# Two graph layers over 4096 nodes on one core: a reciprocal moved behind the first key group, and eleven value tiles written beside the rank sort

## The chip, the cores and the metric

The kernel runs on one core of a Trainium2 chip. A core has five engines that work at the same time, each through its own queue in order: TensorE (PE in the profile, PEld its weight loads), VectorE (DVE), ScalarE (ACT), GpSimd (POOL) and SyncE (SP, which only issues transfers here). They share 16 DMA engines. The metric is the device time of one execution in microseconds (us), as the median of several runs.

## The reference

All numbers are float32. `x` is 4096 x 512, `adj` 4096 x 4096 with very few ones (a chance of 0.000976562 for each entry, made symmetric, with the diagonal set). There are two layers, cut here to what matters:

```python
# layer 0
h = jnp.maximum(_layernorm(x), 0.0)
Q, K, V = (h @ W.T for W in (WQ, WK, WV))       # 8 heads of 64
attn = Q.K / 8 + (Q @ we.T + be)                # per head; only where adj > 0
hard = (attn == max over neighbours) / HEADS
x = x + hard @ V                                # the winning neighbour's values
# layer 1
h = jnp.maximum(_layernorm(x), 0.0)
agg = mask @ h / deg
x = x + relu(concat(h @ W_self + b_self, agg @ W_nb + b_nb) @ W_comb + b_comb)
```

So layer 0 picks for every node and head the neighbour with the best score and adds its values. Layer 1 sums the rows of all neighbours.

## The kernel before, in words

A tile is 128 nodes, so there are 32 (`KT`). The sparse path keeps a table `K_d` in device memory with one row for each node: values V (512 columns), keys K (512), a list of up to 24 neighbours with metadata, and the row of x.

*Stage A, the rows in their own order.* `x` and `adj` are streamed tile by tile. Each tile gets its layernorm, its transposed normalized rows (`hT`, kept in a large buffer `room`, tag `hT_R`), keys, and its neighbour list out of packed adjacency words. The 15 odd tiles below 31 (`EARLY_V`) get their values as they pass. The other 17 are `late_v`: their `hT` stays in `room` and their values are multiplied later. `room` also lends three spare stretches to the stream for rows of `adj`; the third begins at `END_R` and has 2048 columns.

*Ranks.* At the end of stage A (L1000 to L1083) the nodes are sorted by degree, with one-hot products on TensorE. `perm` (L1083) holds the sorted order. `more_values(n)` (L999) writes `n` late tiles here: four matmuls each into `pv` (L627; the profile has two records for one), a scaling copy on ACT into `vs` (L833), and a transfer into the V columns of `K_d`. Before the change it writes 4 tiles behind the rank's prefix sums and 1 behind the rank products (`SOON` is 5), from a pool of three buffers. Those 12 tiles that come after the ranks have had zeros written into their V columns first by SP (L992), since a gather could touch them.

*Stage B, 32 turns.* The loop from L1521 runs from i = -5 to 31 with one sorted tile a turn. Turns are of two kinds. In an `apart` turn the gathers fetch keys only, and the winners' values are fetched later by eight gathers (`value_gathers`, `o`). In a `fused` turn the gathers fetch keys and values together, and the winners' values are picked on DVE. The tiles with most neighbours come first; turns 0 to 3 are apart, later the kinds alternate, and the last ones are fused. A turn uses the engines so:

- POOL: indirect gathers by line 1097, first the row tile (`km`, five turns ahead), then one gather for each neighbour slot (`kg`, or `room` in a fused turn), then value gathers.
- PE: transposes (L1132), the query `q` (L627), and the products `pg` (L627) and `pr` (L1343, L1345) of layer 1.
- DVE: `xo` (L1283: row plus winners' values), then `scores` over key groups, a first of one slot and then of four (multiply L1218, reduce L1221), then the winners (L1237 to L1276).
- ACT: the statistics of `xo` up to the square root of the variance (L1290 to L1293), and the normalization `layer1_norm` (L1310 to L1314).

The layer-1 work of a tile is spread over four turns by the table `plan`: statistics and norm at turn i, transpose at i + 1, products at i + 2, and at i + 3 the `move`: ACT copies `pg` into `gs` (L1351), DVE writes `own` (L1357, called inside `scores` behind the first group of four), and POOL scatters `gs` into `G_d` (L1113). From turn 28 on, two tiles' statistics share a turn.

The reciprocal of the deviation (L1308) is the first line of `layer1_norm`, which stands behind `winners`:

```python
if i >= 0:
    scores(turns[i], lambda: late(layer1_out, "move", i))
late(scatter, "move", i)
...
on(winners, i)
if i < KT - 2:
    late(layer1_norm, "stats", i)
```

*Order.* Both stages are under a manual schedule: the instructions of each engine stand in the order of the program, and semaphores between them follow from reads and writes of the same data. For gathers and writes that touch different columns of `K_d`, `declare_no_dep` says so: the list `beyond` holds gathers that skip the V columns, the list `written` the value writes.

*Stage C, the dense part.* The first eight sorted tiles (`DENSE`) are summed by matmuls over all rows of `G_d` (`da`, L1637); the other tiles gather `G_d` and reduce on DVE. Output follows.

Of the kernel before, what the change touches and what calls it, by code (L numbers as in the profile page):

```python
# [9 lines left out]
F32 = mybir.dt.float32  # L10
# [8 lines left out]
P = 128  # L19
D = 512  # L20
# [517 lines left out]
def sparse_path(  # L538
# [4 lines left out]
    nc = tc.nc  # L543
    N = x.shape[0]
    KT = N // P
# [36 lines left out]
    late_v = [t for t in range(KT) if t not in EARLY_V]  # L582
    RING = 3
    SOON = 5
    room = wp.tile([P, KT * D], F32, tag="hT_R", name="room")
    HALF_R = KT * D // 2

    def hT(t):
        if t in EARLY_V:
            at = EARLY_V.index(t) % RING * D  # L590
        else:
            k = late_v0.index(t)
            at = (RING + k) * D if k < SOON else HALF_R + (k - SOON) * D
        return room[:, at : at + D].rearrange("p (c q) -> p c q", q=P)

    late_v0 = list(late_v)

    END_R = HALF_R + (len(late_v) - SOON) * D
    spare = [
        room[:, at : at + N // 2]  # L600
        for at in (HALF_R - N, HALF_R - N // 2, END_R)
    ]
    assert (RING + SOON) * D <= HALF_R - N and END_R + N // 2 <= KT * D

# [24 lines left out]
    with ExitStack() as pa:  # L629
# [7 lines left out]
        psm = pa.enter_context(tc.tile_pool(name="spsm", bufs=4, space=PSUM))  # L637
# [3 lines left out]
        st = [dict() for _ in range(KT)]  # L641
# [183 lines left out]
        def values(t, ps):  # L825
            pv = ps.tile([P, D], F32, tag="pm", name="pv")
            project(pv, hT(t), ws["wv"])
            return pv

        def values_out(t, pv, pool, eng):  # L830
            vs = pool.tile([P, D], F32, tag="gs", name="vs")

            nc.scalar.activation(vs, pv, AF.Copy, scale=1.0 / H)  # L833
            return eng.dma_start(K_d[ts(t, P), 0:D], vs)
# [111 lines left out]
        for t in range(KT):  # L946
# [30 lines left out]
            if t - 1 in BATCHES[1:]:  # L977
                if decoding:
                    decode_some(99)
                k = BATCHES.index(t - 1)  # L980
# [4 lines left out]
        for b in range(4):  # L985
            n = (KT - FROM_X) * P // 4
# [3 lines left out]

        for t in late_v[SOON:]:
            nc.sync.dma_start(K_d[ts(t, P), 0:D], zero)  # L992
# [2 lines left out]
            nc.sync.dma_start(b, bias.rearrange("(c p) -> p c", p=P))  # L995
        load_fold(1)
        l3.close()
        fo = pa.enter_context(tc.tile_pool(name="sfo", bufs=3))

        def more_values(n):  # L1000
            for t in late_v[:n]:
                values_out(t, values(t, psm), fo, nc.scalar)
            del late_v[:n]


# [32 lines left out]
        )  # L1038
        for k in range(2):
            nc.vector.tensor_tensor(acc[:, ts(k, HF)], pps[k], acc[:, ts(k, HF)], ALU.add)  # L1040
        more_values(4)
        nc.vector.tensor_tensor(acc, acc, ohf, ALU.mult)
        nc.vector.tensor_reduce(
            degc, acc.rearrange("p (b t) -> p t b", b=BINS), AX.X, ALU.add
# [27 lines left out]
        for t in range(KT):  # L1072
            nc.tensor.matmul(
                pp, ohp[:, t, :], tk[:, t], start=(t == 0), stop=(t == KT - 1)
            )
        more_values(SOON - 4)
        decode_some(99)
        words_top(KT - 1)
        decoding = decode(BATCHES[-2], KT - BATCHES[-2])
# [6 lines left out]
    with ExitStack() as pb:  # L1086
# [5 lines left out]
        psm = pb.enter_context(tc.tile_pool(name="spsm2", bufs=3, space=PSUM))  # L1092
# [11 lines left out]
                for w in written:  # L1104
                    tc.declare_no_dep(last[0].ins, w.ins, reason="other columns")

        written, beyond = [], []

        def put_rows(dst, r, src):
            if puts and puts[-1] is last[0]:  # L1110
# [25 lines left out]
        st = [dict() for _ in range(KT)]  # L1136

        def rows(r):

            if r in wide:  # L1140
                k = (wide.index(r) + 3) % OWNS
                own = big[:, OWN0 + k * VKX : OWN0 + (k + 1) * VKX]
                gather(own, K_d[:, :], perm[:, r : r + 1])
                km = own[:, D:VKX]
                st[r]["own"] = own
            else:
                km = xp.tile([P, ROWX], F32, tag="km", name="km", bufs=8)
                gather(km, K_d[:, :], perm[:, r : r + 1], D)
            st[r].update(km=km, xg=km[:, M_X:ROWX])
# [62 lines left out]
        def scores(r, within):  # L1212

            s = st[r]
            sc = bp.tile([P, LIST, H], F32, tag="sc", name="sc", bufs=1)
            for kk, g0, g in s["kg"]:
                pr = bp.tile([P, GRP, D], F32, tag="pr", name="pr", bufs=1)
                nc.vector.tensor_tensor(  # L1218
                    pr[:, :g, :], s["q"].unsqueeze(1).to_broadcast([P, g, D]), kk, ALU.mult
                )  # L1220
                nc.vector.tensor_reduce(  # L1221
                    sc[:, g0 : g0 + g, :],
                    pr[:, :g, :].rearrange("p g (h d) -> p g h d", h=H), AX.X, ALU.add,
                )
                if g0:
                    within()
                    within = lambda: None
            s["sc"] = sc
# [50 lines left out]
        def layer1_stats(r, by_vector=False):  # L1279
# [21 lines left out]
            nc.scalar.activation(rs, v, AF.Sqrt)  # L1301
            s.update(xo=xo, mv=mv, v=v, rs=rs)

        def layer1_norm(r):
            s = st[r]
            if "sq" in s:
                xo, q = s["xo"], s["sq"]
                nc.vector.reciprocal(q[:, 4:5], q[:, 2:3])  # L1308

                nc.scalar.activation(q[:, 5:6], q[:, 4:5], AF.Square)  # L1310
                nc.scalar.activation(q[:, 5:6], q[:, 5:6], AF.Identity, bias=three, scale=q[:, 3:4])
                nc.scalar.activation(q[:, 6:7], q[:, 4:5], AF.Copy, scale=q[:, 5:6])
                nc.scalar.activation(q[:, 7:8], q[:, 6:7], AF.Copy, scale=q[:, 0:1])
                nc.scalar.activation(s["hn"], xo, AF.Relu, bias=q[:, 7:8], scale=q[:, 6:7])  # L1314
                return
            xo, mv, v, rs = (s[k] for k in ("xo", "mv", "v", "rs"))
            nc.vector.reciprocal(rs, rs)

            newton(nc, bp, v, rs, 1, 1)
            nb = bp.tile([P, 1], F32, tag="nb1", name="nb1")  # L1320
            nc.vector.scalar_tensor_tensor(nb, mv[:, 0:1], -1.0, rs, ALU.mult, ALU.mult)
            hn = bp.tile([P, D], F32, tag="hn1", name="hn1", bufs=3)
            nc.scalar.activation(hn, xo, AF.Relu, bias=nb, scale=rs)
            s["hn"] = hn
# [68 lines left out]
        def fold_bias():  # L1393
            for pm in biased:
                nc.vector.tensor_tensor(bb, pm, bb, ALU.add)
# [29 lines left out]
        turns = apart[:FIRST]  # L1425
        left, last_tiles, m = apart[FIRST:], fused[-3:], KT - FIRST - 3
        n = m - len(left)
# [7 lines left out]
        OWNS = (KT * D - OWN0) // VKX  # L1435


        wide = [r for r in fused if r not in last_tiles and pos[r] > 7]
# [19 lines left out]
        i = 0  # L1458
        while ready:
            ripe = sorted(e for e in ready if e[0] <= i)  # L1460
            for e in ripe[: 2 if i >= KT - 4 else 1]:
                ready.remove(e)
                r = e[2]
# [15 lines left out]
        def late(step, kind, i, *args):  # L1479

            out_ = []
            for r in turns:
                if plan[kind].get(r) == i:
                    out_ += step(r, *args) or []
            return out_
# [22 lines left out]
        for i in range(-5, KT):  # L1508


            if i == -3:
                load_fold(0)
            if i == 0:
                load_bias()
            if i == 1:
                wS = wp.tile([P, NC, D], F32, tag="w_b", name="swS")
                wN = bp.tile([P, NC, D], F32, tag="swN", name="swN", bufs=1)
            a, b = on(key_gathers, i), late(value_gathers, "value", i)
            while a or b:
                for q, n in ((a, max(1, round(len(a) / max(1, len(b))))), (b, 1)):  # L1520
                    for g in q[:n]:  # L1521
                        gather(*g)
                    del q[:n]
            on(rows, i + 5)
            late(layer1_move, "move", i)
            on(query_copy, i + 2)
            late(layer1_copy, "layer1", i)
            early = [r for r in tail if plan["turn"][r] == i - 1]
            for r in early:
                tail_turn(r)  # L1530
            if i >= 0 and turns[i] in fused:
                own_values(turns[i])
            late(layer1_stats, "stats", i, i >= KT - 2)
            if i >= KT - 2:
                late(layer1_norm, "stats", i)
            on(query_norm, i + 4)
            on(query, i + 1)
            for part in between.get(i, ()):
                fold(*part)
            late(layer1, "layer1", i)  # L1540
            for r in early:
                tail_product(r)
            if i in (-1, 0):
                n = 6 if i < 0 else KT
                for t in late_v[:n]:
                    w = values_out(t, values(t, psm), bp, nc.sync)
                    for g in beyond:
                        tc.declare_no_dep(w.ins, g.ins, reason="other columns")
                    written.append(w)
                del late_v[:n]  # L1550
            if i == max(between) + 1:
                fold_bias()
            if i >= 0:
                scores(turns[i], lambda: late(layer1_out, "move", i))
            late(scatter, "move", i)
            if i == KT - 2:
                wg = dense_words()
                gsl = [gp.tile([P, GRP, D], F32, tag="kg", name="gs") for _ in range(2)]
# [3 lines that stand above are left out]
            on(query_turn, i + 3)  # L1562
            late(layer1_turn, "turn", i)
            for r in early:
                tail_move(r)
# [14 lines left out]
        r = 0  # L1580
        while r < KT:
# [6 lines left out]
            r = e  # L1588
# [17 lines left out]
    with ExitStack() as pd:  # L1606
# [83 lines left out]
        for r in range(DENSE, KT):  # L1690
            n = CAPS[r] - 1
# [68 lines left out]
```

## Time and profile before

| what | value |
|---|---|
| median of three runs | 1306.7 us (1304.51, 1306.7, 1310.19) |
| the profiled execution's own time | 1449.11 us |
| its span, and mean granted TensorE clock | 1447.4 us, 0.859 |
| DVE layer-1 wait at turn 3: idle before the reciprocal at 515.17 us | 31.68 us, released by ACT L1292 |
| L627 `pv`, all 256 matmuls: busy, mean | 119.0 us, 617 ns |
| L1097 `kg` gathers, 177: busy, mean | 170.1 us, 961 ns |
| L1637 `da`, 512 matmuls: busy, mean | 241.8 us, 628 ns |

The profiled execution is 142 us longer than the median. In the profile's clock row a 9 stands for a slice in which TensorE had full clock; where the digit is lower, its matmuls run longer. A row of the timeline gives start, busy time, engine, line and operation; in square brackets stand the idle time of the engine before it and what ended that. A "L" number is a line of the kernel before.

### The profile page before, as it was taken

To read this page: it belongs to the slowest core of one execution; us is meant where nothing else is said; L and a number is where in the kernel's file an instruction comes from. 1 tells how busy PE (TensorE), PEld (TensorE's weight loads), DVE (VectorE), ACT (ScalarE), POOL (GpSimd) and SP (SyncE) were. 2 spreads that over 40 slices of the span, in tenths; PEclk is the share of its full clock that TensorE was granted. 3 is DMA by queue.
4 is the path that set the end of the run, shared out by engine and by line. 5 is a ranking of instruction groups with operands and counts; after the bars stand their busy time and mean duration, and the time that the engine had idled before them with its cause. 6 is when DMAs were issued, how large, how long until landed. Compare 5 with 4: busy or idle time off the path is not lost. (4 is left out here: it accounts for less than half of the span.)

```text
span 1447.4 us, 10779 instructions
## 1 busy us (share of the span) xinstructions
PE 1053.6 (73%) x2918; PEld 484.7 (33%) x2918; DVE 994.0 (69%) x1666; ACT 420.9 (29%) x862; POOL 773.9 (53%) x910
## 2 busy tenths in 40 slices
PE   5998989565495457666787719466978597996972
PEld 3554555232142123222233303122433243442431
DVE  5568786984566279887787749566764464964985
ACT  5787768311020043223233304233431000000000
POOL 2322322236627666666766665466443757574774
PEclk9999999886798678878888868788999898996985
DMA  9999998396735567777877775576652997575873
GB/s 364 420 419 420 420 357 314 121 331 198 209 108 153 149 197 227 226 234 228 234 228 234 211 240 171 181 219 194 197 182 93 307 347 254 196 257 186 275 260 114
DMA packets 109222, 350.09 MB, mean 242 GB/s; under 512 B 18064, under 2 KB 18064, under 8 KB 100960
## 3 DMA queue, kind: packets, MB, share of 16 engines
q0 software_dynamic: 63376, 208.23, 46.5%
q1 hardware_dynamic: 40416, 131.35, 23.5%
q10 hardware_dynamic: 5360, 9.73, 2.0%
q8 instruction: 25, 0.41, 0.1%
q14 instruction: 45, 0.37, 0.1%
HBM read 285.25 MB, written 68.19 MB: 244 GB/s over the span
## 5 line engine op out<-in xcount | busy, mean ns | idle before, releaser
L1637 PE MATMUL da<-gk,mk 128*128 128x512 f32 x512 | 241.8, 628 | 51.0 <-issue 36.1
L627 PE MATMUL pg<-swN,hT 128*128 128x512 f32 x216 | 124.0, 728 | 130.7 <-ACT hT L1332 99.9
L1097 POOL DMA_INDIRECT room<-G_d,sidx x174 | 176.7, 1016 | 56.5 <-issue 51.8
L1097 POOL DMA_INDIRECT kg<-K_d,sidx x177 | 170.1, 961 | 64.4 <-issue 52.1
L1221 DVE TENSOR_REDUCE sc<-pr 128x32 f32<-128x2048 f32 (+3 forms) x114 | 183.3, 1608 | 3.9
L627 PE MATMUL q<-wq,hqT 128*128 128x512 f32 x256 | 130.7, 639 | 56.6 <-issue 55.0
L1637 PEld LDWEIGHTS da<-gk,mk 128*128 128x128 f32 x512 | 102.2, 200 | 190.5 <-issue 190.5
L1659 DVE TENSOR_REDUCE acc<-room 128x512 f32<-128x4096 f32 (+5 forms) x23 | 152.3, 6623 | 5.4 <-DMA room<-G_d,sidx 3.9
L1097 POOL DMA_INDIRECT o<-K_d,vi x128 | 123.4, 964 | 60.5 <-issue 60.5
L627 PE MATMUL pv<-wv,room 128*128 128x512 f32 x256 | 119.0, 617 | 18.4 <-ACT vs L833 18.4
L627 PE MATMUL pk<-wk,room 128*128 128x512 f32 x256 | 121.0, 617 | 4.1 <-ACT room L809 4.0
L1097 POOL DMA_INDIRECT room<-K_d,sidx x102 | 97.7, 958 | 42.4 <-issue 24.4
L1218 DVE TENSOR_TENSOR pr<-q,kg 128x2048 f32<-128x2048 f32 (+3 forms) x51 | 102.4, 2007 | 25.2 <-DMA kg<-K_d,sidx 24.1
L627 PEld LDWEIGHTS pg<-swN,hT 128*128 128x128 f32 x216 | 49.0, 236 | 209.9 <-ACT hT L1332 116.0
L1113 POOL DMA_INDIRECT G_d<-gs,perm x32 | 31.7, 990 | 128.6 <-ACT gs L1351 85.8
L1345 PE MATMUL pr<-swS,hT 128*128 128x512 f32 x216 | 99.9, 605 | 0.0
L1218 DVE TENSOR_TENSOR pr<-q,room 128x2048 f32<-128x2048 f32 (+3 forms) x42 | 66.8, 1590 | 43.8 <-issue 29.1
L1254 DVE COPY_PREDICATED o<-best,room 128x512 f32<-128x512 int32 x102 | 74.3, 728 | 32.4 <-issue 16.6
L627 PEld LDWEIGHTS q<-wq,hqT 128*128 128x128 f32 x256 | 49.2, 202 | 108.7 <-issue 107.0
L627 PEld LDWEIGHTS pv<-wv,room 128*128 128x128 f32 x256 | 50.4, 199 | 83.1 <-issue 62.6
L748 ACT ACTIVATE mkt<-adjt,sgb 128x2048 bf16<-128x2048 int32 x37 | 74.2, 2006 | 12.5 <-POOL adjt L669 12.2
L823 POOL DMA_DIRECT2D K_d<-ks x32 | 18.7, 585 | 98.3 <-DVE ks L818 96.1
(221 smaller groups left out, 1500.5 us busy)
## 6 DMA issues: line engine op xcount, KB each, us to landing
adjt<-adj_dram SPq DMA_DIRECT2D x37, 1024.0 KB
room<-adj_dram SPq DMA_DIRECT2D x27, 1024.0 KB
x<-X_d SPq DMA_DIRECT2D x32, 512.0 KB
xt<-x_dram SPq DMA_DIRECT2D x32, 256.0 KB
K_d<-ks POOLq DMA_DIRECT2D x32, 256.0 KB
X_d<-xo SPq DMA_DIRECT2D x32, 256.0 KB
X_d<-own SPq DMA_DIRECT2D x32, 256.0 KB
gk<-G_d ACTq DMA_DIRECT2D x16, 512.0 KB
```

Source lines behind the costliest of these rows:

```text
L627: nc.tensor.matmul(dst, h[:, c, :], w[:, c, :], start=(c == 0), stop=(c == NC - 1))
L748: nc.scalar.activation(mk, st[t]["adj"][j], AF.Sigmoid, bias=sgb, scale=400.0, accum_out=degs[:, t, j : j + 1],)
L823: nc.gpsimd.dma_start(K_d[ts(t, P), D : 2 * D], ks)
L1097: last[0] = nc.gpsimd.indirect_dma_start(out=dst, out_offset=None, in_=src, in_offset=bass.IndirectOffsetOnAxis(ap=idx, axis=0), element_o ...
L1113: new = nc.gpsimd.indirect_dma_start(out=dst, out_offset=bass.IndirectOffsetOnAxis(ap=perm[:, r : r + 1], axis=0), in_=src, in_offset=None,)
L1218: nc.vector.tensor_tensor(pr[:, :g, :], s["q"].unsqueeze(1).to_broadcast([P, g, D]), kk, ALU.mult)
L1221: nc.vector.tensor_reduce(sc[:, g0 : g0 + g, :], pr[:, :g, :].rearrange("p g (h d) -> p g h d", h=H), AX.X, ALU.add,)
L1254: nc.vector.copy_predicated(s["o"].rearrange("p (h d) -> p h d", h=H), best[:, k, :].bitcast(I32).unsqueeze(2).to_broadcast([P, H, HD]), b ...
L1345: nc.tensor.matmul(pr, s["hT1"][:, c, :], wS[:, c, :], start=False, stop=(c == NC - 1))
L1637: nc.tensor.matmul(dacc[r], masks[s][:, h, r, :], keys[s][:, h, :], start=(s == 0 and h == 0), stop=(s == NPL - 1 and h == 1),)
L1659: nc.vector.tensor_reduce(acc, g[:, 0:n, :].rearrange("p n f -> p f n"), AX.X, ALU.add)
```

## The change

It has three parts.

1. *Value tiles.* `more_values` now writes 8 tiles behind the prefix sums and 3 behind the rank products, 11 in all (`BESIDE`), instead of 4 and 1. They are copied into four slots of 512 columns in the third spare stretch of `room`, in turn, and no longer into the pool of three buffers. Their writes are put into `written`, so the gathers that skip the V columns need not wait for them. The six tiles left are written two a turn in turns -2, -1 and 0, where before twelve were written, six in turn -1 and six in turn 0.
2. *Reciprocal.* It leaves `layer1_norm` and becomes `layer1_inverse`. For turns below 30 it is called inside `scores`, behind the first group of four key slots and ahead of `layer1_out`.
3. *Own slots.* The formula of the slot of a fused row is written in another way; with 11 rows in `wide` it yields the same slots.

In the order of the program, DVE's eight copies of the bias (`fb`, L1372) stand ahead of `perm` (L1083) after the change.

```diff
+    BESIDE = 11
...
-        def values_out(t, pv, pool, eng):
-            vs = pool.tile([P, D], F32, tag="gs", name="vs")
+        def values_out(t, pv, pool, eng, vs=None):
+            if vs is None:
+                vs = pool.tile([P, D], F32, tag="gs", name="vs")
...
-        fo = pa.enter_context(tc.tile_pool(name="sfo", bufs=3))
+        written = []
 
         def more_values(n):
             for t in late_v[:n]:
-                values_out(t, values(t, psm), fo, nc.scalar)
+
+                at = END_R + len(written) % 4 * D
+                written.append(
+                    values_out(t, values(t, psm), None, nc.scalar, room[:, at : at + D])
+                )
             del late_v[:n]
...
-        more_values(4)
+        more_values(8)
...
-        more_values(SOON - 4)
+        more_values(BESIDE - 8)
...
-        written, beyond = [], []
+        beyond = []
...
-                k = (wide.index(r) + 3) % OWNS
+                k = (wide.index(r) - len(wide) + 4) % OWNS
...
+        def layer1_inverse(r):
+            q = st[r]["sq"]
+            nc.vector.reciprocal(q[:, 4:5], q[:, 2:3])
+
         def layer1_norm(r):
             s = st[r]
             if "sq" in s:
                 xo, q = s["xo"], s["sq"]
-                nc.vector.reciprocal(q[:, 4:5], q[:, 2:3])
...
-            if i in (-1, 0):
-                n = 6 if i < 0 else KT
+            if i in (-2, -1, 0):
+                n = 2
...
+            def within():
+                if i < KT - 2:
+                    late(layer1_inverse, "stats", i)
+                late(layer1_out, "move", i)
+
             if i >= 0:
-                scores(turns[i], lambda: late(layer1_out, "move", i))
+                scores(turns[i], within)
```

## The prediction

> **What bounds the kernel now.** I read four views in this order: the page's clock row, the waits from 330 to 430 us and from 500 to 1000 us, the timeline at the places these waits name, and sums over windows.
>
> ```profile
> span 1447.4 us, 10779 instructions
> PE 1053.6 (73%) x2918; PEld 484.7 (33%) x2918; DVE 994.0 (69%) x1666; ACT 420.9 (29%) x862; POOL 773.9 (53%) x910
> PEclk9999999886798678878888868788999898996985
> ...
> L1113 POOL DMA_INDIRECT G_d<-gs,perm x32 | 31.7, 990 | 128.6 <-ACT gs L1351 85.8
> ```
>
> No engine is full. The clock row is full for eight slices (the stage that streams adj) and ragged after. That matters for the frame: the profiled execution took 1449.11 us, the median of three is 1306.7, so 142 us of the profile are not in the runs that count. They must sit where the clock was low. The last row says that the scatters of the layer-1 products wait on ACT's copy `gs`, more than on anything else.
>
> ```profile
> POOL o L1097 <- issue: 22.1, 2, 21.8
> POOL kg L1097 <- ACT smeta L1154: 10.7, 1, 10.7
> DVE pr L1218 <- remote: 13.6, 1, 13.6
> ```
>
> ```profile
> ACT q L1310 <- DVE q L1308: 71.7, 10, 15.3
> POOL G_d L1113 <- ACT gs L1351: 63.5, 9, 14.9
> DVE q L1308 <- ACT q L1292: 31.7, 1, 31.7
> ```
>
> The first three rows are 330 to 430 us, the others 500 to 1000 us (total, times, longest). At the start of the turns POOL stands still for 21.8 us before the first value gather: it needs all V rows written. Later ACT waits ten times for the reciprocal (71.7 us) and POOL nine times for `gs` behind it.
>
> ```profile
> 298.40 13.90 PE L627 MATMUL pv<-wv,room 128*128 128x512 f32 x32
> 425.42 0.95 POOL L1097 DMA_INDIRECT o<-K_d,vi  x1 [21.77 <-issue]
> ...
> 704.11 0.29 ACT L1292 ACTIVATE q<-q,c 128x1 f32<-128x1 f32 x1
> 716.86 0.15 DVE L1308 RECIPROCAL q<-q 128x1 f32<-128x1 f32 x1
> 717.04 0.20 ACT L1310 ACTIVATE q<-q 128x1 f32<-128x1 f32 x1 [11.40 <-DVE o L1254]
> ...
> 1035.48 0.21 DVE L1308 RECIPROCAL q<-q 128x1 f32<-128x1 f32 x2
> 1037.82 0.69 DVE L1283 TENSOR_TENSOR xo<-km,o 128x512 f32<-128x512 f32 x1 [2.13 <-ACT hn L1314]
> 1039.70 0.56 ACT L1351 COPY gs<-pg 128x512 f32<-128x512 f32 x1
> 1040.55 1.00 POOL L1113 DMA_INDIRECT G_d<-gs,perm  x1 [8.22 <-ACT gs L1351]
> 1058.09 1.00 POOL L1113 DMA_INDIRECT G_d<-gs,perm  x1 [9.01 <-ACT gs L1351]
> ```
>
> The first line gives the price of a value tile at full clock: 13.90 / 4 = 3.47 us. The square root of a turn is ready at 704.40, its reciprocal runs at 716.86, because it stands behind the winners. At 1035 the chain reciprocal, norm on ACT, `gs`, scatter is plain, and DVE's next `xo` waits for it too.
>
> ```profile
> 449.00:1018.00 569.00, 352.54 (x829) 148.68 (x828) 406.50 (x495) 166.42 (x433) 369.82 (x385) 0.80 0.70 210
> 1018.00:1114.00 96.00, 80.75 (x213) 35.30 (x212) 62.00 (x121) 31.50 (x75) 35.02 (x42) 0.95 0.46 157
> 1114.00:1447.00 333.00, 263.76 (x560) 110.25 (x558) 221.59 (x110) 0.00 (x0) 210.77 (x216) 0.87 0.72 242
> ```
>
> Columns: window, length, busy PE, PE load, DVE, ACT, POOL (and counts), clock, DMA share, GB/s. In the middle turns POOL comes nearest to full: an indirect DMA is 0.95 to 0.96 us and 0.30 before the next, 1.257 us apiece, so 384 x 1.257 = 482.7 of 569 us.
>
> **What the Trainium skill says.** "TensorE: Matmul & The Clock Gate", What's actually happening: TensorE starts at half clock and returns to it after an idle window of about 3.4 us. The trace agrees that waits and low clock go together (clock 0.80 in the middle turns), but a low stretch costs more here than a factor of two: one value tile ran from 360.9 to 381.9 and the next to 396.6, 21.0 and 14.7 us against 3.47. "Perfetto Trace Analysis", Tensor Engine Instruction (MATMUL, LD_WEIGHTS): a matmul's end is estimated, and ACT, DVE and GpSimd are strict FIFO. It fits: records of `pv` end near 363 us while ACT's copy waits until 381.9, and `gs` stays behind a norm it has nothing to do with. "DMA: Bandwidth & Descriptors", Issuing engines are not separate DMA queues: another issuer saves only the issue time. The trace has 0.33 us (ACT) and 0.32 to 0.34 us (SP) for the value writes, so moving writes to ACT is nearly free.
>
> **The change, part by part.** The base is the profile's durations replayed at full clock, since the median is 142 us below. I split these 142: the dense end has at least (1 - 0.87) x 333 = 43 us of lost clock, call it 55 as the loss is more than linear; the start of the turns about 25; some 62 remain for 449 to 1114. POOL's idle time in the middle turns, 569 - 482.7 = 86 us, is then only 20 to 25 at full clock.
>
> *Values, start.* Before, 5 tiles run beside the ranks and 12 in turns -1 and 0 (6 and 6). After, 11 beside the ranks and 6 later, 2 a turn. The four more tiles ahead of the rank products delay TensorE: 4 tiles 298.4 to 312.3 become 8 tiles, to 326.2 (8 x 3.47 = 27.8). `r_tk`, behind eight value copies on ACT, is done about 328.1, the 1.87 us of rank products about 330. DVE's eight `fb` copies (1.18 us) now stand ahead of `perm` and still wait for the last metadata write; they ran at 332.51, so `perm` is ready at about 334.15 instead of 329.8. The first `km` gather, at 335.31 before, starts about 2.9 us after its last wait: 337.0, **+1.7 us**. The first `q` comes 5 us later (355 for 350), but turn 0 is bound by its 23 gathers, so it ends +2.9.
>
> What returns: at full clock before, 6 tiles end at 370.4, `q` of turn 1 at 374.6, the other 6 at 395.2, the last write has landed at about 400. POOL reaches its first value gather at 393.4 and waits 6.6. After, with two tiles a turn, `q` of turn 1 is done about 366 and the last write landed about 378: POOL doesn't wait. Its gathers of turn 2 end at 418.7 for 424: **-5 us**, the 1.7 included. In the profile's clock it would be some 25, as the 21.8, 10.7 and 13.6 above all hang on tiles at low clock.
>
> The slots in the adjacency's spare room replace three buffers by four: a write takes 3.3 us to land and a slot is used again after 4 x 3.47 us. I cost it at nothing; if that cover went, a tile would wait 1 to 3 us. Six fewer SP writes are worth 6 x 0.33 us on a queue nobody waits for. The own-slot formula gives the same slots, at nothing.
>
> *Reciprocal, middle turns.* 0.15 us of DVE moves from behind the winners to behind the first key group; `own` stands directly behind it. ACT gets the norm's input up to 12 us earlier (704.4 for 716.86) and the whole norm, 717.04 to 719.2 or 2.1 us, is out of `gs`'s way. Of what is late next: in the pair of turns from 694.98 to 738.21 (43.2 us), POOL has 30 DMAs, 37.7 us, and one wait for `gs`, 4.75 at 726.94, where TensorE ran at clock 0.50. There the product is late as well, and an earlier norm brings nothing to it. So at full clock these waits are small before the change, and POOL's issue is what remains. Of the 20 to 25 us left I take **-4** (bounds 0, as POOL may be full anyway, and -20).
>
> The moved reciprocal adds a wait: behind it stand `own` and the remaining key groups, and for them `scatter` doesn't wait but the next `xo` does. Its input is ready at `xo` + 3.2 to 4.4 us without trouble, the first group ends at `xo` + 6.7: no wait. Bounds 0 and +16 per turn (rival D).
>
> *Reciprocal, tail.* Window two has clock 0.95, so its waits are real in all runs. Square roots are ready at 1027.1 and 1029.1; the first group ends at 1028.8. The reciprocals come at about 1029.2 for 1035.48; norms (2 x 2.1) and `gs` 1033.8 for 1039.7. The scatter waits of 8.22 and 9.01 shrink by about 6 each, and DVE's 2.13 + 1.32 before `xo` go. What is late next is TensorE's `pg`. Half of the two 6 us reach the end, plus 3.4: **-9** (8 to 13). From i = 30 the old place stays.
>
> The dense stage has no edit: 0. Sum: -5 - 4 - 9 = -18, so 1306.7 - 18 = **1288.7, taken as 1288.5 us**. Against the profile's own execution the same steps read 25 + 25 + 12 = 62, 1449.1 to 1387, of which the median holds the 18.
>
> **Rivals.**
> A, the forecast: -18, own range 1277 to 1300.
> B, the low clock at the tiles and `gs` is in the median runs too, if less: for it speaks that every turn has TensorE pauses of several us that bring it on; against it the 142 us. Then half of the 62 and the tail's 9: -40, **1266**.
> C, the gathers' issue bounds all turns: what ACT and TensorE get earlier waits again for POOL, and two turns earlier at the start only fill slack. For it 482.7 of 569 us. What stays is half of the tail: -4, **1303**.
> D, slower: the reciprocal blocks DVE. At 483.49 DVE waited 31.68 us for the square root at its old place, with the turn's work already done. At the new place, the rest of the key groups and the winners (15 to 17 us) would come after such a wait. Two such turns cost 31, against them 18 less 3 that other waits absorb: +10 to +16, **1317**. It decides as soon as ACT's square root is later than the first group's end by over 6 us (DVE's slack: 569 - 406 = 163 us over 27 turns). Against it: the wait stands once in the profile, in a stretch of low clock.
>
> **How the numbers follow.** A 0.50, B 0.21, C 0.17, D 0.12. Half a per cent, 6.5 us, is about what a measurement of this kernel can tell from no change: 1300.2 to 1313.2. A lies almost wholly below it, B wholly; C inside it; D mostly above. Faster 0.73, same 0.16, slower 0.11. The range goes from B's lower part, 1258, to C's upper bound, 1308; left out are most of D and the lower third of B, about 0.19.
>
> **What would show it.** Right: in the profile after, POOL's wait before the first `o` gather is under 7 us; `perm` about 4 us later; the reciprocal starts within 1 us of the first group's end; the waits of ACT L1310 on the reciprocal fall to under 15 us; scatters near 1040 and 1058 wait under 4 us. Wrong: DVE waits for L1292 of over 6 us in more than two turns (D); scatter waits that stay with TensorE's `pg` as releaser (C); or a drop of over 30 us in the median (B).

## The result and the profile after

The changed kernel takes 1294.4 us (median of 4, 1291.45 to 1295.04), the kernel before 1307.7 us (median of 4) beside it. The ratio is 0.9897, 95% interval 0.9878 to 0.9916: 13.3 us less, where 18 were forecast. A ratio leaves out runs over 1.5% above the fastest of the same kernel, so it is not always the quotient of two medians.

The same kernel before has a median of 1307 us on two chips (numbers 8 and 1 in the record) and of 1442 and 1447 us on two others (0 and 4), with a lower granted TensorE clock there (0.85 to 0.86 for 0.89 to 0.90). The first profile, of 1449.11 us, is of the second kind. The runs of the result and the profile after are of the first; their chip is not on record. So before and after are compared below on a second profile of the kernel before, the run f0 (1305.33 us).

The page after, with its span, its busy row and its clock row:

```profile
span 1293.3 us, 10762 instructions
PE 1025.0 (79%) x2918; PEld 483.8 (37%) x2918; DVE 993.5 (77%) x1666; ACT 422.1 (33%) x862; POOL 776.3 (60%) x910
PEclk9999998988898868887889988988898799999985
```

Busy times are nearly those of the kernel before in its second profile (VectorE 993.8 us there, POOL 773.0, TensorE 1019.9): the change moves work. The group of scatters, from the list of groups by line (busy, mean ns, idle time ahead of them and what ended it):

```profile
L1119 POOL DMA_INDIRECT G_d<-gs,perm x32 | 32.4, 1013 | 40.0 <-ACT gs L1511 24.4 <-ACT gs L1360 8.8 <-issue 4.4
```

The scatters' idle time was 128.6 us in the first profile and is 40.0 here. But most of that fall isn't the change's. The same row of the kernel before in its second profile:

```profile
L1113 POOL DMA_INDIRECT G_d<-gs,perm x32 | 32.1, 1003 | 47.0 <-ACT gs L1502 23.8 <-ACT gs L1351 15.8 <-issue 4.8
```

It is 47.0 us: some 80 us of the first profile's waits are not there in an execution of 1305 us. The change takes the part behind the copy L1351 (L1360 after) from 15.8 to 8.8; the part behind the other copy, of the last tiles, stays (23.8 and 24.4). The waits of the changed kernel, 330 to 430 us and 500 to 1000 us:

```profile
DVE pr L1224 <- PE q L628: 26.9, 1, 26.9
POOL o L1103 <- issue: 2.7, 9, 0.3
```

```profile
ACT q L1319 <- DVE q L1312: 86.2, 23, 7.3
POOL G_d L1119 <- ACT gs L1360: 8.8, 4, 7.9
```

POOL's wait before the value gathers is gone (nine times 0.3 is the usual spacing). ACT still waits 86.2 us for the reciprocal (273.3 in the second profile before), but what matters is who waits behind it: POOL, 8.8 us. The first `q` is what VectorE now waits for longest.

The page shows what the moved reciprocal does to TensorE. The products `pg` of layer 1, before (second profile) and after:

```profile
L627 PE MATMUL pg<-swN,hT 128*128 128x512 f32 x216 | 131.6, 766 | 101.2 <-ACT hT L1332 101.2
```

```profile
L628 PE MATMUL pg<-swN,hT 128*128 128x512 f32 x216 | 97.1, 592 | 0.0
```

Before, TensorE paused 101.2 us in all ahead of `pg`, and a matmul of it took 766 ns on average; after, it doesn't pause there and a matmul takes 592 ns. The pause now stands ahead of the queries `q` (36.7 us before, 143.0 after), and they are slower instead (628 and 788 ns). The reciprocal alone does the same (run f1 below: 592 ns without a pause), and with the reciprocal moved in the late turns only (run g1) `pg` stays at 740 ns. So the pause is moved and not removed.

The tail, timeline of the changed kernel, where the forecast put most of the gain:

```profile
912.83 0.21 DVE L1312 RECIPROCAL q<-q 128x1 f32<-128x1 f32 x2
...
919.77 1.32 POOL L1119 DMA_INDIRECT G_d<-gs,perm  x1 [0.30 <-issue]
931.56 0.16 DVE L1312 RECIPROCAL q<-q 128x1 f32<-128x1 f32 x1 [2.87 <-ACT q L1298]
936.49 1.00 POOL L1119 DMA_INDIRECT G_d<-gs,perm  x1 [7.87 <-ACT gs L1360]
```

and of the kernel before in its second profile:

```profile
923.49 0.20 DVE L1308 RECIPROCAL q<-q 128x1 f32<-128x1 f32 x2
...
928.54 1.00 POOL L1113 DMA_INDIRECT G_d<-gs,perm  x1 [4.68 <-ACT gs L1351]
946.70 1.00 POOL L1113 DMA_INDIRECT G_d<-gs,perm  x1 [9.63 <-ACT gs L1351]
```

The pair of reciprocals runs 10.7 us earlier from the start of the execution, but part of that lies far ahead of it: counted from POOL's DMA 397 in the table below it is 5.7 us. The scatter behind the pair doesn't wait any more (4.68 before). The next one waits 7.87 instead of 9.63: here VectorE itself waits 2.87 us at the new place of the reciprocal.

POOL issues the same 690 indirect DMAs in the same order in all these kernels, so the start of the same one can be compared. Start times in us, from the traces (before is its second profile):

| POOL's DMA | before | values alone | reciprocal alone | both |
|---|---|---|---|---|
| last metadata write of stage A | 334.6 | 333.5 | 333.5 | 331.8 |
| indirect DMA 1, first `km` | 339.8 | 340.6 | 338.7 | 338.9 |
| 49, turn 2 | 406.2 | 404.3 | 406.7 | 403.1 |
| 397, turn 21 | 848.1 | 847.5 | 847.4 | 843.1 |
| 469, behind the scatter of turn 30 | 953.0 | 952.4 | 946.7 | 942.8 |
| span | 1303.6 | 1303.9 | 1299.0 | 1293.3 |

The first row is ahead of the change's first visible effect on POOL and differs by up to 2.8 us from run to run; differences of rows are safer than rows. Of the 10.3 us between the spans of before and both, 2.8 are in it. The steps, from before to both: metadata to `km` +1.9 (5.2 to 7.1); to DMA 49 -2.2; to 397 -1.8; to 469 -5.3; the rest -0.1. They sum to -7.5 us, against 13.3 between the medians: each column is a single execution, and the remainder isn't assigned to any stage.

### The profile page after: what moved, and what is told of

The parts are those of the page before. It is cut to its first block, busy times and chain, and to the rows that moved or that the text cites. A ratio compares the mean times of both kernels' runs of the same rounds, so it can differ in the third digit from the quotient of the medians.

```text
span 1293.3 us, 10762 instructions
## 1 busy us (share of the span) xinstructions
PE 1025.0 (79%) x2918; PEld 483.8 (37%) x2918; DVE 993.5 (77%) x1666; ACT 422.1 (33%) x862; POOL 776.3 (60%) x910
## 4 chain that ended last, share of the span: by engine, by line
DVE 21%; DMA 21%; PE 20%; POOL 19%; issue 14%; ACT 3%; SPq 0%; DVEq 0%; POOLq 0%; ACTq 0%
POOL room L1103 9%; PE pv L628 6%; DMA room<-K_d,sidx 6%; DVE pr L1224 6%; DMA room<-G_d,sidx 5%; PE pk L628 5%; POOL kg L1103 5%; DMA kg<-K_d,sidx 4%; POOL o L1103 3%; DVE sc L1227 3%; PE pr L1354 2%; PE pw L768 2%; DMA adjt<-adj_dram 2%; ACT mkt L749 2%; PE pg L628 2%
## 5 line engine op out<-in xcount | busy, mean ns | idle before, releaser
L628 PE MATMUL q<-wq,hqT 128*128 128x512 f32 x256 | 161.2, 788 | 143.0 <-DVE pr L1224 143.0
L1652 PE MATMUL da<-gk,mk 128*128 128x512 f32 x512 | 221.4, 595 | 15.8 <-DMA gk<-G_d 15.8
L1103 POOL DMA_INDIRECT room<-G_d,sidx x174 | 180.3, 1036 | 58.0 <-issue 46.3
L1652 PEld LDWEIGHTS da<-gk,mk 128*128 128x128 f32 x512 | 97.8, 191 | 139.4 <-issue 139.0
L628 PEld LDWEIGHTS q<-wq,hqT 128*128 128x128 f32 x256 | 62.5, 256 | 221.1 <-DVE pr L1224 124.2
L628 PE MATMUL pv<-wv,room 128*128 128x512 f32 x256 | 115.9, 604 | 0.0
L628 PE MATMUL pg<-swN,hT 128*128 128x512 f32 x216 | 97.1, 592 | 0.0
L1296 ACT ACTIVATE hn<-xo 128x512 f32<-128x512 f32 x29 | 18.2, 629 | 192.6 <-DVE xo L1289 185.3
L628 PEld LDWEIGHTS pk<-wk,room 128*128 128x128 f32 x256 | 48.3, 199 | 54.4 <-issue 48.8
```

The source lines that it names most:

```text
L628: nc.tensor.matmul(dst, h[:, c, :], w[:, c, :], start=(c == 0), stop=(c == NC - 1))
L1103: last[0] = nc.gpsimd.indirect_dma_start(out=dst, out_offset=None, in_=src, in_offset=bass.IndirectOffsetOnAxis(ap=idx, axis=0), element_o ...
L1296: nc.scalar.activation(junk, xo, AF.Copy, scale=-1.0 / D, accum_out=q[:, 0:1])
L1652: nc.tensor.matmul(dacc[r], masks[s][:, h, r, :], keys[s][:, h, :], start=(s == 0 and h == 0), stop=(s == NPL - 1 and h == 1),)
```

## The experiments

The first four ran on chip 0, where the kernel before takes 1442.4 us.

**The kernel before again (e0).**

> The kernel before, once more, for a profile whose clock is that of the runs that count. The theory of the prediction (full-clock replay): POOL's wait before the first value gather, 21.8 us in the first profile, is 5 to 9 us; POOL's idle time between 449 and 1018 us is 20 to 30 us instead of 86; the scatters in the tail still wait 7 to 9 us each for gs. The rival (low clock is in all runs): POOL's wait before the first value gather stays above 15 us.

It took 1452.7 us at clock 0.855, and POOL waited 18.3 us before the first value gather. This is the rival's figure, but it can't decide: the execution is of the long kind itself.

**Reciprocal alone (e1).** The kernel before with this edit only:

```diff
+        def layer1_inverse(r):
+            q = st[r]["sq"]
+            nc.vector.reciprocal(q[:, 4:5], q[:, 2:3])
...
-                nc.vector.reciprocal(q[:, 4:5], q[:, 2:3])
...
+            def within():
+                if i < KT - 2:
+                    late(layer1_inverse, "stats", i)
+                late(layer1_out, "move", i)
```

> The kernel before with the reciprocal moved and nothing else. The theory of the prediction: 9 us in the tail and 4 in the middle turns, so 1307.7 - 13 = about 1295 (ratio 0.990). Rival 1 (the values carry the gain): no change, 1304 to 1308. Rival 2 (the moved reciprocal blocks VectorE while the value tiles still crowd TensorE in turns -1 and 0): slower than before, over 1310.

Measured: 1463.8 us, ratio 1.0141 (1.0101 to 1.0181), slower. The waits of VectorE for the square root between 440 and 1000 us, with the edit and then in the kernel before (e0):

```profile
DVE q L1306 <- ACT q L1292: 121.8, 6, 42.2
```

```profile
DVE q L1308 <- ACT q L1292: 32.4, 1, 32.4
```

There are six waits for one, and from POOL's DMA 49 to its DMA 397 the turns take 553.2 us for 514.6. This fits the mechanism of rival D. But the trace is of an execution of 1495.8 us, the longest of six, so neither figure is the size of the median's loss. What is shown is that VectorE is caught at the new place; that this makes the 1.4% is argued, and the run h1 below speaks against it as the only cause.

**Values alone (e2)**, the changed kernel with the line put back:

```diff
                 xo, q = s["xo"], s["sq"]
+                nc.vector.reciprocal(q[:, 4:5], q[:, 2:3])
...
-                if i < KT - 2:
-                    late(layer1_inverse, "stats", i)
```

> The changed kernel with the reciprocal put back behind the winners. The theory of the prediction: 5 us, about 1302 (ratio 0.996). Rival 1 (the values carry the gain): 1294 to 1297. If the two single edits add up, their gains sum to the 13.3 us of the whole change.

Measured: 1457.1 us as the median of six, which scatter from 1432.1 to 1468.5. The ratio, 0.9971 (0.9906 to 1.0037), rests on two of them: no difference to be told.

**Reciprocal in the late turns (e3).**

```diff
-                if i < KT - 2:
+                if 26 <= i < KT - 2:
                     late(layer1_inverse, "stats", i)
...
-                late(layer1_norm, "stats", i)
+                late(layer1_norm, "stats", i, i < 26)
```

(The added argument makes the norm begin with the reciprocal, as before.)

> The changed kernel with the reciprocal behind the first key group in turns 26 to 29 only, behind the winners in turns 0 to 25. The theory of the prediction: the tail gives 9 of the reciprocal's 13 us, so this is some 4 us over the changed kernel, about 1298. Rival (the gain of the reciprocal lies in the middle turns): as slow as with the reciprocal put back everywhere.

Measured: 1438.2 us, ratio 0.9964 (0.9915 to 1.0012). The loss of the run with the reciprocal alone isn't there. But two things differ from that run, the reciprocal's place in the middle turns and the value tiles, so it doesn't say which of them matters.

**On a chip where the kernel before takes 1307 us.** The next three ran on chip 8 (median of the kernel before 1306.7 us), the first being the kernel before once more (f0).

> The kernel before once more. If it takes about 1307 us here, as in the runs that gave the verdict, its profile replaces the first one: POOL's wait before the first value gather 5 to 9 us, POOL's idle time between 449 and 1018 us 20 to 30 us, scatters of the tail waiting 7 to 9 us for gs. If it takes about 1440 us, this chip grants TensorE less, as in the first four runs.

It took 1305.33 us. The wait before the value gathers, timeline:

```profile
403.73 0.95 POOL L1097 DMA_INDIRECT o<-K_d,vi  x1 [6.28 <-issue]
```

It is 6.28 us, where the replay at full clock had 6.6. But from DMA 49 to DMA 397 POOL takes 441.8 us; at the 1.257 us apiece of the prediction the 348 DMAs between them are 437.4, so 4.4 us are left idle and not 20 to 30, and the longest two waits are 1.50 and 1.45. Of the two scatters in the tail one waits 4.68 us, under the 7 to 9 expected, the other 9.63.

The reciprocal alone, with the edit of e1 (f1):

> The kernel before with the reciprocal moved and nothing else, where the kernel before takes about 1307 us. The theory of the prediction: ratio 0.990 (9 us tail, 4 us middle turns). Rival 1 (the values carry the gain): 0.997 to 1.000. Rival 2 (the moved reciprocal blocks VectorE while twelve value tiles crowd TensorE and ScalarE in turns -1 and 0): over 1.005, as on the chip with less TensorE clock, where it was 1.014.

Measured: 1298.2 us, ratio 0.9927 (0.9908 to 0.9946). Both rivals are out; the gain is somewhat under the forecast 0.990. VectorE's waits for the square root between 440 and 1000 us are one of 2.8 us. In the traces POOL gains 5.6 us from DMA 397 to 469 (105.0 to 99.4) and 1.2 from 49 to 397.

The values alone, with the edit of e2 (f2):

> The changed kernel with the reciprocal back behind the winners, where the kernel before takes about 1307 us. The theory of the prediction: 0.996. Rival 1: 0.988 to 0.992. If the single edits add up, the product of both ratios is that of the whole change, 0.990.

Measured: 1306.1 us, ratio 0.9990 (0.9977 to 1.0003): no gain to be told, where 0.996 was forecast. The product of the two single ratios is 0.9917, the whole change has 0.9897; the intervals overlap. POOL's stalls in the values-alone kernel:

```profile
340.62 1.08 POOL L1103 DMA_INDIRECT km<-K_d,perm  x1 [6.30 <-issue]
367.99 0.95 POOL L1103 DMA_INDIRECT kg<-K_d,sidx  x1 [1.14 <-DVE pr L1224]
399.25 0.95 POOL L1103 DMA_INDIRECT kg<-K_d,sidx  x1 [2.65 <-issue]
```

The 6.28 us before `o` are gone; in their place stand 1.14 and 2.65 for key buffers and 1.9 more before the first `km` (6.30 for 4.42). The turns from DMA 49 to 397 also take 1.4 us more than in the kernel before (443.2 for 441.8).

The next four ran on chip 1, where the kernel before takes 1307.25 us. The first is the changed kernel with the reciprocal at its new place in turns 26 to 29 only, with the edit of e3 (g1):

> The changed kernel with the reciprocal behind the first key group in turns 26 to 29 only. Where the kernel before takes about 1307 us. If the tail carries the reciprocal's gain: within 3 us of the changed kernel, 1294 to 1297, since POOL's waits for gs between 449 and 900 us, which come back, sum to about 3 us. If the middle turns carry it: 1301 or more.

Measured: 1298.1 us, ratio 0.9925 (0.9906 to 0.9944), 3.7 us over the changed kernel's 1294.4; the intervals overlap (0.9878 to 0.9916 there). From DMA 49 to DMA 397 POOL takes 444.0 us here and 440.0 in the changed kernel. Two waits, of 2.61 and 1.80 us where the changed kernel's longest is 0.74, account for most of it. The larger:

```profile
595.96 0.99 POOL L1119 DMA_INDIRECT G_d<-gs,perm  x1 [2.61 <-ACT gs L1362]
```

So by the medians the late turns carry 8 us (1306.1 with the values alone, 1298.1 here) and the others about 4. By POOL's DMAs the late turns carry 5.4 (397 to 469: 105.0 with the values alone, 99.6 here); another 1.9 us lie behind DMA 469, a stretch that is 1.8 us longer in f1 than in f0.

**`perm` first (g2):** `fb` behind the scores of turn 0.

```diff
-            if i == 0:
-                load_bias()
...
             if i >= 0:
                 scores(turns[i], within)
+            if i == 0:
+                load_bias()
```

> The changed kernel with the eight bias copies (fb) behind turn 0's scores, so that perm no longer stands behind them. If perm behind fb costs what the prediction said: the first km gather comes 1.7 us earlier (2.8 us after the last metadata write has landed instead of 4.5), and the time is 1 to 2 us lower, 1292 to 1294. Rival (another wait takes its place): no change.

Measured: 1294.4 us, ratio 0.9903 (0.9882 to 0.9924), as the changed kernel. The first `km` comes 1.8 us sooner behind POOL's metadata write (4.5 us of idle time for 6.3), and the waits for key buffers take it back:

```profile
367.30 0.95 POOL L1103 DMA_INDIRECT kg<-K_d,sidx  x1 [2.28 <-DVE pr L1224]
399.63 0.95 POOL L1103 DMA_INDIRECT kg<-K_d,sidx  x1 [3.65 <-issue]
```

2.28 + 3.65 against 1.68 + 2.65: the rival was right.

**Eight tiles beside the ranks (g3).**

```diff
-    BESIDE = 11
+    BESIDE = 8
...
-        more_values(BESIDE - 8)
...
-            if i in (-2, -1, 0):
-                n = 2
+            if i in (-1, 0):
+                n = 4 if i < 0 else KT
```

> The changed kernel with 8 tiles beside the ranks and none behind the rank products; 4 of the other 9 in turn -1 behind the first query and 5 in turn 0. If the three tiles behind the rank products and the two of turn -2 are what holds the first query back (362.8 us in the changed kernel's profile, against 354 before): the first q is done near 352, POOL's waits of 1.7 and 2.6 us for key buffers at 365 and 395 go, no wait of over 1 us before the first value gather: 3 to 4 us lower, about 1291. Rival (turn 0's gathers hide the late query wholly): no change; or slower by the 6 us wait before the value gathers, if the last values land late.

Measured: 1292.5 us, ratio 0.9888 (0.9868 to 0.9909). The first `q` is done at 355.7 us, not near 352; in this execution the first `km` came 1.7 us later than in the changed kernel's. VectorE's first scores:

```profile
355.68 0.69 DVE L1223 TENSOR_TENSOR pr<-q,km 128x512 f32<-128x512 f32 x1 [18.11 <-PE q L628]
```

They start 15.1 us behind the first `km`; in the changed kernel it is 362.82 - 338.91 = 23.9. POOL has no wait over 0.6 us from there to the tail, and its first `o` comes 58.2 us behind `km` for 61.7. Those 3.5 us are what was expected; 1.9 show in the median, which the intervals can't separate from none.

**Turn 29 put in another order (g4).**

```diff
-                junk = bp.tile([P, D], F32, tag="hn1", name="hn1", bufs=3)
+                if r == [t for t in turns if plan["stats"][t] == KT - 3][-1]:
+                    junk = s["o"]
+                else:
+                    junk = bp.tile([P, D], F32, tag="hn1", name="hn1", bufs=3)
...
             late(layer1_move, "move", i)
+            if i == KT - 2:
+                late(layer1_norm, "stats", i - 1)
...
-            if i < KT - 2:
+            if i < KT - 3:
                 late(layer1_norm, "stats", i)
```

> The changed kernel with two edits in turn 29: the second tile's statistics use the room of its o instead of a fourth use of the three hn1 buffers, and its norms stand behind the gs copy of turn 30. If VectorE's wait of 2.9 us for the square root at 931 us and POOL's wait of 7.9 us for gs at 936 us both come from that buffer and that order: VectorE's wait goes, the scatter at 936.5 comes 3 to 7 us earlier, and the time is 3 to 5 us lower, about 1290. Rival (TensorE's products pg of turns 30 and 31 are the next wait): the scatter comes earlier, the time stays.

Measured: 1291.8 us, ratio 0.9874 (0.9852 to 0.9895), the lowest median of all, though its interval overlaps that of the changed kernel. Its scatters:

```profile
930.41 1.00 POOL L1119 DMA_INDIRECT G_d<-gs,perm  x1 [0.30 <-ACT q L1323]
...
957.78 0.97 POOL L1119 DMA_INDIRECT G_d<-gs,perm  x1 [7.05 <-ACT gs L1514]
```

The wait of 7.87 is gone, and so is VectorE's of 2.87. The next scatter in want of TensorE's product waits 7.05 (4.23 in the changed kernel): both theories hold in part. Of the 8.4 us that POOL gains from DMA 397 to 469 (99.7 to 91.3), 3.5 are lost again behind it (350.5 to 353.9).

**The three edits together (h1)**, g2, g3 and g4.

> Three edits of the changed kernel together: 8 tiles beside the ranks with 4 and 5 later, turn 29's statistics room and norm order, and fb behind turn 0's scores. The single gains over the changed kernel's 1294.4 us were 1.9, 2.6 and 0. If POOL is the bound from the first km gather to 925 us once nothing stops it, the 1.7 us of an earlier perm now reach the end too: 1.9 + 2.6 + 1.7 = 6.2 less, about 1288. If the fb copies at their later place hold VectorE up in turn 0 again: a POOL wait of over 1 us before 400 us, and 1290 or more.

This ran on chip 4, where the kernel before takes 1446.7 us: 1443.6 us, ratio 0.9994 (0.9962 to 1.0026). Whether the gains add up at 1307 us was so not tried. VectorE waits 84.9 us in 8 waits at the moved reciprocal (32.4 in 1 in the kernel before, e0), and yet the kernel isn't slower: the turns from DMA 49 to 397 take 518.2 us, 3.6 more than in e0, where e1 took 38.6 more. So such waits alone don't make e1's 1.4%. Whether the moved values take the loss away, or this run's other edits, was not tried.

## Why the prediction was right, point by point

The direction, the range and the part that carries most of the gain were right. By the medians one term was too large, that of the values; by POOL's DMAs all three were.

- *The frame.* That 142 us of the first profile go with its low clock and are absent from the median was the choice on which all rests. The second profile bears it out: the scatters' idle time falls from 128.6 to 47.0 us with no edit. Rival B, in which the waits are in the median too, fell. But the 142 us were split wrongly. Set side by side, the two profiles of the kernel before differ by 26 us from the first `km` to DMA 49 (25 forecast), by 28 behind the last scatter (55 forecast) and by 94 in the turns between (62). So hardly any idle time was left for the middle turns.
- *Values, -5.* This is the term that was mis-sized: the ratio of 0.9990 is 1.3 us alone, and no change lies within its interval. The replay's two entries were right: `perm` behind `fb` cost 1.9 us (1.7 forecast) and the wait before the value gathers was 6.28 (6.6) and went. The step that failed is "turn 0 is bound by its 23 gathers, so it ends +2.9": from the metadata to DMA 49 the values alone gain 0.9 us, not 5. The first scores came 9.3 us later behind the first `km` (23.9 for 14.6) and not 3.3 (5 less the 1.7), since the queries' first transposes began at 349.1 with their input ready at 344.65, and two tiles stood ahead of the first query. Turn 0 has four key buffers; with VectorE so late, POOL waited for them, 1.1 and 2.7 us. The run g3 takes the tiles away and with them both waits. That the transposes waited for ACT's copies of the last tiles (the second ends at 348.99) is inferred from the order of events, not tried alone. With the reciprocal moved as well, the values bring 1298.2 - 1294.4 = 3.8 us. In the traces the 1.4 us that the values alone cost in the middle turns are gone when the reciprocal moves too (443.2 and 440.0); the rest isn't settled, and the intervals allow for no difference.
- *Reciprocal, middle, -4.* 3.7 us by g1's median, 4.0 by POOL's own count against g1. That the size came out is in part luck: "20 to 25 us" of idle time at full clock was too much. POOL has 4.4 us there in the kernel before and is otherwise full, as rival C said, and against that kernel the whole change saves 1.8 (441.8 to 440.0). The 4.0 come about since, with the values moved and the reciprocal not, POOL is idle for 6.6 us there by the same reckoning (g1), and with both moved for 2.6.
- *Reciprocal, tail, -9.* 8 us by the medians of f2 and g1; in the traces POOL gains 5.3 to 5.6 us from DMA 397 to 469 in each of three pairs (before to both, before to reciprocal alone, values alone to g1). The mechanism is in the two timelines: the reciprocals 5.7 us earlier, counted from DMA 397 (6.3 forecast), the first scatter's wait gone. "The scatter waits shrink by about 6 each" was right for the first only in kind (4.68 to 0.30), and for the second wrong (9.63 to 7.87), since a second square root of the turn was late; g4 takes that wait away.
- *The added wait.* "No wait" holds at 1307 us but for one of 2.9 us. Where the kernel before takes 1442 us the reciprocal alone was 1.4% slower, as rival D has it. The whole change was not run there; nearest is h1, three more edits on top of it, which was not slower.
- *The signs.* POOL's wait before `o` is under 7 us, but so it was before the change at 1307 us (6.28): this sign could not tell. `perm` came 4.4 us later behind the metadata write, as forecast, and the reciprocals follow the first group directly but for the one wait. ACT's waits for the reciprocal did not fall under 15 us (86.2): ACT is not what the kernel waits for, so their sum says little. Of the two scatters one waits under 4 us, the other 7.87. Of the signs of being wrong, VectorE's waits of over 6 us did not come at 1307 us. C's is there in part: the last scatters still wait 24.4 us for copies that stand behind `pg`, as before the change (23.8).
- *One reading.* "A low stretch costs more than a factor of two" isn't shown. The 14.7 us stand between two of ACT's copies, and a query's transposes and products lie between them too; in the 21.0 us TensorE's records end early and ACT's copy waits for something that the trace doesn't name.

## What to carry to other kernels

Before costing a change, ask how the profiled execution stands to the runs that count: a profile 10% over the median shows waits that the median doesn't have, and the same durations replayed at full clock gave 6.6 us for a wait that then measured 6.28. But how the difference splits over the stages needs a second profile: the guess here left 20 to 25 us where 4.4 were. When work is moved ahead of the first use of a pipeline, follow it to the buffers that let the stages run apart: the gathers kept coming until the four key buffers were full, and then POOL waited for the later query. A short instruction moved forward in an engine's queue stalls all that stands behind it where its input is late, so ask how late that can be (2.9 us in the profile at 1307 us, up to 41.9 in h1); the same move was 0.7% faster on one chip and 1.4% slower on another. And compare executions from one event that both have, not from their start: 10.7 us were 5.7.

## What was not expected of the hardware

The same kernel took 1306.7 us on chip 8 and 1442.4 on chip 0, 10% apart, while the mean granted clock of the two profiles differed by 5% only (0.902 and 0.855). All runs of one kind had clocks of 0.89 to 0.90, all of the other 0.85 to 0.86, so the clock tells which kind a profile is, but not what it costs. Whether it is the chip or the time at which it ran, four chips with one set of runs each can't say.

At 1307 us a low stretch costs little: eight matmuls of `q` took 6.33 us at one place of the changed kernel, 3.60 at another. In the run e0 two of ACT's copies of value tiles are 21.8 us apart, where the price of a tile is 3.47. What held them up isn't shown: TensorE's records end long before, and its next tile waits for the copy.
